# Neighbour marks instead of indices, one-hots on ScalarE, one softplus function, and three steps in other slots

## The chip, the cores and the metric

The kernel runs on one core of one Trainium2 chip. That core has TensorE (PE, matrix products), VectorE (DVE), ScalarE (ACT), GpSimd (POOL) and SyncE (SP), which here only starts transfers (DMAs). The engines run side by side, each through its own queue in order, and wait for each other by semaphores. The metric is the device time of one execution in microseconds (us). Three executions of the kernel before took 13008.24, 13020.53 and 13022.36 us; the median is 13020.53.

## The reference

The input is an image batch x of 16 x 96 x 64 x 64. Layer 0 is a graph convolution over windows of 8 x 8 pixels, layer 1 a stack of two Mamba blocks (state-space scans) over the 4096 pixels of each image, with a normalisation over the batch at the end. Cut to what matters here:

```python
# layer 0, in each window of 64 nodes
idx = knn_idx(nodes, 9)                       # the 9 nearest nodes of each node, itself included
feat = concat([x_i, x_j - x_i])               # for each neighbour j of i
h = gelu(affine(feat @ ew + eb)).max(axis=2)  # the greatest over the 9 neighbours
y = affine(conv1x1(h, fc2_w, fc2_b)) + x

# layer 1, twice for each image: one Mamba block
xs, z = split(layernorm(seq) @ in_w)
xc = silu(causal_conv4(xs) + conv_b)
dt, Bm, Cm = split(xc @ xproj_w)
delta = softplus(dt @ dt_w + dt_b)            # 192 channels
dA = exp(delta * A);  dBx = delta * Bm * xc   # 16 states per channel
h[l] = dA[l] * h[l-1] + dBx[l]
y = (sum_s h * Cm + Dp * xc) * silu(z)
seq = seq + y @ out_w
```

The order of the neighbours does not enter the result, since the maximum is taken over them.

## The kernel before, in words

**Items and slots.** Layer 1 is cut into 256 items: 16 images x 2 blocks x 8 pieces of 512 pixels. The states are taken two at a time (2 x 64 partitions), so an item has 8 slots, p = 0 to 7, each with 128 partitions x 3 x 512 values. The main loop (L871) writes 2048 slots one after the other. In each slot DVE does one scan (L911), adds the carried state to the first column (L907), and makes the input of the next slot's scan, db = u * bt (L734 in `times_b`). TensorE spreads B over the partitions (bt, L729 in `bcast`, into a single PSUM buffer), and sums the states into y (`folded`, L745 and L747). ACT makes da = exp(delta * A) two slots ahead (L708 in `chosen`), with four buffers of da. POOL multiplies the scan's result by C (L943). SP fetches C for each slot (ct, L701, in `chosen`, four buffers).

**Preparing an item.** `norm` and `prelude` are generators; the main loop runs one step of each per slot, up to the next `yield`. `norm(n + 2)` begins in slot 0 of item n, `prelude(n + 2)` in slot 4. The prelude's steps before the change are: the silu of half the convolution (slot 4), the other half and the gate's silus, then a load of the table with exp and ln (L627, slot 5); the product that holds dt, B and C, copied to `dbl` (slot 6); B and C sent off, the product for delta, its Abs and Relu (L653, L654, slot 7). In the next item: exp and 1 + exp (L656, L658), then ln (L661), minus one (L662) and the splitting of B into three bf16 parts (L665, L667), both in slot 0, which runs the prelude twice (L924, L925); then, on POOL, a correction and two sums that finish the softplus (L672, L674, L676, slots 1 to 3); `delta` is spread by eight DMAs of SP and u = delta * xc is formed on POOL (L679, L681, slot 4); u is spread by eight more DMAs (L684, slot 5). `doubled` issues these eight (L690, L692). Delta is first read by the small exps and by da of the next item's slot 0, which are written two slots ahead; u is first read by the db of the next item's slot 0, which is written in slot 7.

**Carry.** In slot 5 `carry(n + 1)` begins: a product on POOL (L717), an exp on ACT (L719), and in later slots a product with the carried state (L723), which L907 reads.

**Output.** In slot 6 `tail(n - 1)` begins: four matrix products of the gated result with out_w, plus the old sequence (L772 to L777), and a copy on ACT (L781).

**Layer 0.** Each image has 8 rows of 8 windows; a row is handled by `nearest` (distances and neighbours) and `edges` (products, gelu, maximum), also generators. The first four rows are done ahead of the main loop, the next ones quickly in the first items, the rest at one row per two items, in steps between the slots. In `nearest`, DVE finds the eight greatest of a row (L396) and their places (`max_index`, L397, run at the head of the next slot, at L909); SP writes the places to memory (L401). In `edges`, SP reads them back to 64 partitions (L430); POOL compares them with the partition's number for half of the windows (L441), and ACT does the same for the other half with an Abs and a Relu (L443, L444). The result is a one-hot matrix `oh`, with which PE picks the neighbours (L468, L471).

ACT holds one table of functions at a time. Silu, gelu and exp/ln are in different tables; before a function of another table an ACT_TABLE_LOAD stands in its queue.

Of the kernel before, what the change touches and what calls it, by code (L numbers as in the profile page):

```python
# [10 lines left out]
F32 = mybir.dt.float32  # L11
U16 = mybir.dt.uint16
BF16 = mybir.dt.bfloat16
AF = mybir.ActivationFunctionType
# [7 lines left out]
def tile_conv_knn_mamba(ctx: ExitStack, tc: tile.TileContext, w: dict, out: bass.AP):  # L22
# [44 lines left out]
    node = const.tile([NN, 1], F32, name="node")  # L67
    nc.gpsimd.iota(node, pattern=[[0, 1]], base=0, channel_multiplier=1, allow_small_or_imprecise_dtypes=True)
    minus_node = const.tile([NN, 1], F32, name="minus_node")
    nc.vector.tensor_scalar(minus_node, node, -1.0, None, ALU.mult)  # L70
# [237 lines left out]
    def half(h):  # L308
        return slice(h * CB, (h + 1) * CB)
# [21 lines left out]
    def nearest(b, q):  # L331
# [61 lines left out]
        idx = pr.tile([128, NP, KO], U16, tag="idx", name=f"idx_{nm}")  # L393
        for p in range(NP):
            m1 = pr.tile([128, KO], F32, tag="m1", name=f"m1_{nm}_{p}")
            nc.vector.max(m1, scs[:, p, :])  # L396
            opening.append(partial(nc.vector.max_index, idx[:, p, :], m1, scs[:, p, :]))  # L397
            yield SLOT

        idx_d = dram.tile([NP, 128, KO], U16, tag="idx_d", name=f"idxd_{nm}")  # L400
        nc.sync.dma_start(out=idx_d.rearrange("p i k -> i p k"), in_=idx)  # L401
        chosen_of[b, q] = idx_d
# [13 lines left out]
    def edges(b, q):  # L416
# [3 lines left out]
        idx_d = chosen_of.pop((b, q))  # L420
# [7 lines left out]
        for hf in range(2):  # L428
            idb = pr.tile([NN, NP, NN * KO], U16, tag="idb", name=f"idb_{nm}_{hf}", bufs=1)
            nc.sync.dma_start(  # L430
                out=idb.rearrange("j w n -> j (w n)"),
                in_=idx_d.rearrange("(s p) i k -> s (p i k)", s=2)[hf : hf + 1].to_broadcast([NN, NP * NN * KO]),
            )
            yield


            for p in (1, 0):
                ohj = ohs[p][0:NN].rearrange("j w i k -> j w (i k)")
                numbers = idb[:, 2 * p : 2 * p + 2, :]
                if p == 0:  # L440
                    nc.gpsimd.tensor_scalar(ohj, numbers, node, None, ALU.is_equal)  # L441
                else:
                    nc.scalar.activation(ohj, numbers, AF.Abs, bias=minus_node)  # L443
                    nc.scalar.activation(ohj, ohj, AF.Relu, bias=1.0, scale=-1.0)  # L444
                yield
# [119 lines left out]
    made = {}  # L565
    carried = {}
# [26 lines left out]
    def prelude(n):  # L593
# [31 lines left out]
        for part in range(2):  # L625
            project(z_in[i].unsqueeze(1), 1, part, z, 0.0)
        nc.scalar.preload_act_table_set("natural_log_exp_and_others")  # L627
# [13 lines left out]


        e = pr.tile([128, Q + QH], F32, tag="e", name=f"e_{nm}", bufs=1)
        rl = pr.tile([128, Q + QH], F32, tag="rl", name=f"rl_{nm}", bufs=1)
        va = pm.tile([128, Q], F32, tag="mm", name=f"pdta_{nm}")
        nc.tensor.matmul(va, lhsT=dt_w[i][:, :128], rhs=dbl, start=True, stop=True)
        vb = pm.tile([128, QH], F32, tag="mm", name=f"pdtb_{nm}")
        for h in range(2):
            nc.tensor.matmul(
                vb[half(h)], lhsT=dt_w[i][:, 128:], rhs=dbl[:, bass.ts(h, QH)], start=True, stop=True  # L650
            )
        for v, cols in ((va, slice(0, Q)), (vb, slice(Q, Q + QH))):
            nc.scalar.activation(e[:, cols], v, AF.Abs)  # L653
            nc.scalar.activation(rl[:, cols], v, AF.Relu)  # L654
        yield
        nc.scalar.activation(e, e, AF.Exp, scale=-1.0)  # L656
        s1 = pr.tile([128, Q + QH], F32, tag="s1", name=f"s1_{nm}", bufs=1)
        nc.scalar.activation(s1, e, AF.Identity, bias=1.0)  # L658
        yield
        ln = pr.tile([128, Q + QH], F32, tag="ln", name=f"ln_{nm}", bufs=1)  # L660
        nc.scalar.activation(ln, s1, AF.Ln)  # L661
        nc.scalar.activation(s1, s1, AF.Identity, bias=neg1)  # L662
# [9 lines left out]
        nc.gpsimd.tensor_tensor(e, e, s1, ALU.subtract)  # L672
        yield
        nc.gpsimd.tensor_tensor(ln, ln, e, ALU.add)  # L674
        yield
        nc.gpsimd.tensor_tensor(ln, ln, rl, ALU.add)  # L676
        yield
        delta = pr.tile([128, NB3, Q], F32, tag="delta", name=f"delta_{nm}")
        doubled(delta, ln)  # L679
        u = pr.tile([128, NB3, Q], F32, tag="u", name=f"u_{nm}")  # L680
        nc.gpsimd.tensor_tensor(s1, ln, xc, ALU.mult)  # L681
        made[n] = (xc, z, bp, c_d, delta, u)
        yield
        doubled(u, s1)  # L684
# [26 lines left out]
    def carry(n):  # L711
# [4 lines left out]
        d0 = made[n][4][:, :, 0:1].to_broadcast([128, NB3, NPR])  # L716
        nc.gpsimd.tensor_tensor(first, a_neg[i], d0, ALU.mult)  # L717
        yield
        nc.scalar.activation(first, first, AF.Exp)  # L719
# [151 lines left out]
    for m, (n, p) in enumerate(order):  # L871
# [17 lines left out]
        if p == 5 and k + 1 < NQ:  # L889
            going.append(carry(n + 1))  # L890
# [29 lines left out]
        if p == 6 and n:  # L920
            going.append(tail(n - 1))
        if p == 2:
            ahead()
        if p == 0:  # L924
            step_on(preps)  # L925
# [3 lines left out]
        held |= step_on(preps)  # L929
        close_steps()  # L930
# [83 lines left out]
```

## Time and profile before

| | |
|---|---|
| median of three runs | 13020.53 us |
| the profiled execution | 13021.43 us, its span 13019.7 us |
| mean granted clock of TensorE | 0.949 |
| first scan to last scan | begins at 263.3, the last at 12813.5 us |
| one item, in the middle of the run | 48.6 us, 8 slots |
| one item among the first five | about 76 us |
| DVE busy from 800 to 12800 us | 11431 of 12000 us |

In a line of a group the numbers after the shapes are the count, the busy time in us, the mean of one in ns, then how long the engine had been idle just before these instructions, and what ended most of that. A line of the waits has the engine that waited, the one it waited for, the total in us, how often, and the longest. In a line of the timeline stand the start and the length in us, the engine and line, the operation, and how many are merged; SPq is SP's queue as it issues a DMA, and its length there is the time to issue, not the time to land.

### The profile page before, as it was taken

Reading aid. Unit: us, or ns where it says so; the run is one execution under the profiler, and the core shown is the slowest. Engines: PE = TensorE matmul, PEld = TensorE weight load, DVE = VectorE, ACT = ScalarE, POOL = GpSimd, SP = SyncE. Lnnn points to the kernel's source line nnn. Section 1 sums busy time; section 2 is a strip of 40 time slices with the busy share of each in tenths; the row PEclk is TensorE's granted clock in tenths of the full one; section 3 lists DMA queues with packets and bytes.
Section 4 is the critical chain, followed back from the end, with each engine's and each line's share of the span. In section 5 each row is a group of like instructions: output and inputs, shape, how many; then the busy total and the mean of one; then the engine's idle time right before and its main releaser. Section 6 shows DMA issues by size and latency. Waiting matters only on the chain.

```text
span 13019.7 us, 155850 instructions
## 1 busy us (share of the span) xinstructions
PE 11254.7 (86%) x46920; PEld 4359.3 (33%) x46920; DVE 11940.4 (92%) x8270; ACT 10407.8 (80%) x16186; POOL 11686.0 (90%) x8644
## 2 busy tenths in 40 slices
PE   5889889888989989888888888988888888889872
PEld 2333333333333333333333333333333333333320
DVE  2699999999999999999999999999999999999995
ACT  4778888888888888888888888888888888888763
POOL 3699999999999999999999999999999999999993
PEclk8899999999999999999999999999999999999986
DMA  1233333333333333333333333333333333333336
GB/s 38 66 85 95 91 91 93 94 92 89 98 89 90 96 92 90 93 94 89 95 95 87 98 92 90 94 92 93 90 95 92 90 95 93 92 89 97 89 87 261
DMA packets 1031198, 1226.82 MB, mean 94 GB/s; under 512 B 429440, under 2 KB 560910, under 8 KB 1024208
## 3 DMA queue, kind: packets, MB, share of 16 engines
q1 hardware_dynamic: 1026352, 1191.59, 35.2%
q10 hardware_dynamic: 4000, 25.28, 0.5%
q8 instruction: 370, 6.06, 0.2%
q14 instruction: 476, 3.90, 0.1%
HBM read 706.83 MB, written 85.72 MB: 61 GB/s over the span
## 4 chain that ended last, share of the span: by engine, by line
POOL 27%; PE 19%; DVE 18%; ACT 13%; issue 9%; DMA 7%; SPq 6%; POOLq 0%; DVEq 0%; ACTq 0%
POOL hb L943 16%; DVE hb L911 11%; DVE db L734 6%; ACT da L708 5%; PE y L745 3%; SPq L690 2%; SPq L692 2%; DMA ct<-cd 2%; POOL ln L674 2%; PE t L468 2%; PE y L747 1%; PE pj L608 1%; PE t L471 1%; POOL hn L591 1%; POOL ln L676 1%
## 5 line engine op out<-in xcount | busy, mean ns | idle before, releaser
L943 POOL TENSOR_TENSOR hb<-hb,ct 128x1536 f32<-128x1536 f32 x2048 | 7091.9, 3463 | 313.5 <-DVE hb L911 78.4
L911 DVE TENSOR_TENSOR_SCAN hb<-da,db 128x1536 f32<-128x1536 f32 x2048 | 6863.5, 3351 | 216.6 <-ACT da L708 39.4
L708 ACT ACTIVATE da<-delta,a 128x511 f32<-128x511 f32 x6144 | 3937.7, 713 | 28.7 <-DVE hb L911 24.1
L734 DVE TENSOR_TENSOR db<-u,bt 128x1536 f32<-128x1536 f32 x2048 | 3605.3, 1760 | 386.6 <-PE bt L729 266.3
L745 PE MATMUL y<-hb,fold 128*64 128x512 f32 x8192 | 2273.8, 634 | 230.4 <-POOL hb L943 219.7
L476 ACT ACTIVATE da<-t,eb,es 128x512 f32<-128x512 f32 x1536 | 1181.3, 777 | 775.3 <-PE t L468 534.7
L747 PE MATMUL y<-hb,fold 128*64 128x256 f32 x8192 | 1259.5, 386 | 0.0
L729 PE MATMUL bt<-bparts,bsel 128*128 128x512 bf16 x2048 | 828.4, 404 | 462.4 <-DVE db L734 459.3
L468 PE MATMUL t<-oh,vu 128*128 128x512 f32 x2048 | 1012.8, 616 | 27.2 <-ACT da L476 14.1
L747 PEld LDWEIGHTS y<-hb,fold 128*64 128x64 f32 x8192 | 604.2, 141 | 1247.6 <-issue 1247.6
L413 DVE TENSOR_REDUCE hq<-da 128x192 f32<-128x1536 f32 x512 | 890.4, 1739 | 105.4 <-ACT da L476 105.4
L608 PE MATMUL pj<-hn,conv_in 128*128 128x512 f32 x2048 | 932.8, 598 | 0.9 <-POOL hn L591 0.9
L745 PEld LDWEIGHTS y<-hb,fold 128*64 128x64 f32 x8192 | 495.0, 141 | 1278.5 <-issue 528.6
L441 POOL TENSOR_SCALAR oh<-idb,node 64x1024 f32<-64x1024 uint16 x256 | 731.0, 2855 | 117.2 <-DMA idb<-idxd 111.6
L452 PE MATMUL pv<-ewT,y 96*64 96x192 f32 x2048 | 477.6, 360 | 335.2 <-ACT rs L588 253.4
L942 POOL COPY state<-hb 128x3 f32<-128x3 f32 x1792 | 397.5, 222 | 392.3 <-DVE hb L911 359.0
L620 ACT ACTIVATE xc<-pj,conv_b 128x512 f32<-128x512 f32 (+1 forms) x512 | 297.2, 580 | 510.5 <-PE pj L613 397.8
L471 PE MATMUL t<-oh,vu 128*64 128x512 f32 x2048 | 560.4, 626 | 167.0 <-ACT da L476 162.3
L608 PEld LDWEIGHTS pj<-hn,conv_in 128*128 128x128 f32 x2048 | 396.4, 194 | 386.5 <-issue 375.7
L613 PE MATMUL pj<-hn,conv_in 128*64 128x256 f32 x4096 | 514.4, 394 | 0.0
L452 PEld LDWEIGHTS pv<-ewT,y 96*64 96x64 f32 x2048 | 253.0, 143 | 774.4 <-ACT rs L588 358.4
L468 PEld LDWEIGHTS t<-oh,vu 128*128 128x128 f32 x2048 | 373.5, 194 | 402.9 <-issue 290.3
(180 smaller groups left out, 17972.0 us busy)
## 6 DMA issues: line engine op xcount, KB each, us to landing
ct<-cd SPq DMA_DIRECT2D x4096, 128.0 KB
delta<-ln SPq DMA_DIRECT2D x1024, 128.0 KB
u<-s SPq DMA_DIRECT2D x1024, 128.0 KB
idb<-idxd SPq DMA_DIRECT2D x256, 256.0 KB
delta<-ln SPq DMA_DIRECT2D x1024, 64.0 KB
u<-s SPq DMA_DIRECT2D x1024, 64.0 KB
x<-in_x SPq DMA_DIRECT2D x128, 192.0 KB
rn<-r4d SPq DMA_DIRECT2D x128, 192.0 KB
```

The costliest lines, as they stand in the source:

```text
L413: nc.vector.tensor_reduce(out(), g.rearrange("p s (i k) -> p s i k", k=KO), AX.X, ALU.max)
L441: nc.gpsimd.tensor_scalar(ohj, numbers, node, None, ALU.is_equal)
L468: nc.tensor.matmul(t, lhsT=vus[p][:, part, :128], rhs=ohw[part], start=True, stop=True)
L476: nc.scalar.activation(g, t, AF.Gelu, bias=e_b[:, j : j + 1], scale=e_s[:, j : j + 1])
L608: nc.tensor.matmul(ps, lhsT=wt[:, t, :128], rhs=hn[:, off : off + Q], start=(t == 0), stop=(t == taps - 1))
L708: nc.scalar.activation(da[:, c, 1:Q], delta[:, c, 1:], AF.Exp, scale=a_neg[i][:, c, p : p + 1])
L729: nc.tensor.matmul(bt, lhsT=bsel[:, p, :], rhs=made[n][2], start=True, stop=True)
L734: nc.vector.tensor_tensor(db, made[n][5], bt.unsqueeze(1).to_broadcast([128, NB3, Q]), ALU.mult)
L745: nc.tensor.matmul(y[half(h), 0], lhsT=fold, rhs=hb[:, h, :], start=False, stop=(p == NPR - 1))
L747: nc.tensor.matmul(y[half(h), 1, :QH], lhsT=fold, rhs=hb[:, 2, bass.ts(h, QH)], start=False, stop=(p == NPR - 1))
L911: nc.vector.tensor_tensor_scan(*(t.rearrange("p c q -> p (c q)") for t in (hb, das[at], db)), 0.0, ALU.mult, ALU.add)
L943: nc.gpsimd.tensor_tensor(hb, hb, ct.unsqueeze(1).to_broadcast([128, NB3, Q]), ALU.mult)
```

## The change

- **Neighbours as marks.** `max_index` becomes `match_replace`: DVE overwrites the eight greatest in the table of scores by a mark of 2^20. PE transposes the marked table by products with the identity (eight of 64 x 64 for a row of windows), and ACT makes it 0 or 1 in bf16 (`mt`). Nothing is written to memory and read back.
- **One-hots by ScalarE.** For each one-hot PE forms ranks: the number of marks before a node, by a product with a fixed triangular matrix, plus 100 for a mark itself, less 100 + k (`ranks`). Where that is zero the node is the k-th neighbour. ACT takes the Abs into `off`, and then Relu(1 - |.|), in two halves (`onehot`). POOL's comparison goes, and so do ACT's two passes over the places.
- **Softplus as one function.** `AF.Softplus` stands for the Abs, Relu, Exp, two Identity, Ln and the three POOL operations. It has a table of its own. `press` holds it, with its products and the eight DMAs of delta; it is run in slot 5, after the silus of the following prelude and ahead of the table load for exp and ln.
- **u** is then formed in slot 6 and spread in slot 7; the second prelude step in slot 0 goes.
- **Carry** begins in slot 6, and its POOL product and exp become three exps with a scale per partition.
- **The output projection** (`tail`) begins in slot 7.

```diff
@@ nearest
-            opening.append(partial(nc.vector.max_index, idx[:, p, :], m1, scs[:, p, :]))
+            opening.append(partial(nc.vector.match_replace, scs[:, p, :], m1, scs[:, p, :], MARK))
             yield SLOT
-        idx_d = dram.tile([NP, 128, KO], U16, tag="idx_d", name=f"idxd_{nm}")
-        nc.sync.dma_start(out=idx_d.rearrange("p i k -> i p k"), in_=idx)
-        chosen_of[b, q] = idx_d
+        ps = pm.tile([128, NP, NN], F32, tag="mm", name=f"mp_{nm}")
+        for h in range(2):
+            for p in range(NP):
+                nc.tensor.matmul(
+                    ps[half(h), p, :], lhsT=scs[half(h), p, :], rhs=ident[half(h), half(h)], start=True, stop=True
+                )
+        mt = pr.tile([128, NP, NN], BF16, tag="mt", name=f"mt_{nm}", bufs=3)
+        nc.scalar.activation(mt, ps, AF.Relu, bias=neg1, scale=2.0 / MARK)
+        chosen_of[b, q] = mt
@@ edges
-            idb = pr.tile([NN, NP, NN * KO], U16, tag="idb", name=f"idb_{nm}_{hf}", bufs=1)
-            nc.sync.dma_start(out=idb..., in_=idx_d...)
-            yield
-            for p in (1, 0):
...
-                if p == 0:
-                    nc.gpsimd.tensor_scalar(ohj, numbers, node, None, ALU.is_equal)
-                else:
-                    nc.scalar.activation(ohj, numbers, AF.Abs, bias=minus_node)
-                    nc.scalar.activation(ohj, ohj, AF.Relu, bias=1.0, scale=-1.0)
-                yield
+            def ranks(p):
+                ps = pm.tile([128, NN, KO], F32, tag="mm", name=f"rk_{nm}_{hf}_{p}")
+                nc.tensor.matmul(ps, lhsT=sel0, rhs=krow.rearrange("o (i k) -> o i k", k=KO), start=True, stop=False)
+                marks = mt[:, 2 * hf + p, :].unsqueeze(2).to_broadcast([128, NN, KO])
+                nc.tensor.matmul(ps, lhsT=before, rhs=marks, start=False, stop=True)
+                off = pr.tile([128, NN, KO], BF16, tag="off", name=f"off_{nm}_{hf}_{p}")
+                nc.scalar.activation(off, ps, AF.Abs)
+                return off
+            def onehot(p, off):
+                for h in range(2):
+                    nc.scalar.activation(ohs[p][0:NN, h], off[half(h)], AF.Relu, bias=1.0, scale=-1.0)
+            off = ranks(1)
+            yield
+            onehot(1, off)
+            off = ranks(0)
+            yield
+            onehot(0, off)
+            yield
@@ prelude
+        while pressed:
+            pressed.pop(0)()
         nc.scalar.preload_act_table_set("natural_log_exp_and_others")
...
-        for v, cols in ((va, slice(0, Q)), (vb, slice(Q, Q + QH))):
-            nc.scalar.activation(e[:, cols], v, AF.Abs)
-            nc.scalar.activation(rl[:, cols], v, AF.Relu)
-        yield
-        nc.scalar.activation(e, e, AF.Exp, scale=-1.0)
...
-        nc.gpsimd.tensor_tensor(e, e, s1, ALU.subtract)
-        yield
-        nc.gpsimd.tensor_tensor(ln, ln, e, ALU.add)
-        yield
-        nc.gpsimd.tensor_tensor(ln, ln, rl, ALU.add)
-        yield
...
-        doubled(delta, ln)
+        def press():
+            va = pm.tile([128, Q], F32, tag="mm", name=f"pdta_{nm}")
+            nc.tensor.matmul(va, lhsT=dt_w[i][:, :128], rhs=dbl, start=True, stop=True)
...
+            nc.scalar.activation(sp[:, :Q], va, AF.Softplus)
+            nc.scalar.activation(sp[:, Q:], vb, AF.Softplus)
+            doubled(delta, sp)
+        pressed.append(press)
-        nc.gpsimd.tensor_tensor(s1, ln, xc, ALU.mult)
         made[n] = (xc, z, bp, c_d, delta, u)
-        yield
-        doubled(u, s1)
+        for _ in range(5):
+            yield
+        while pressed:
+            pressed.pop(0)()
+        nc.gpsimd.tensor_tensor(up, sp, xc, ALU.mult)
+        yield
+        doubled(u, up)
@@ carry
-        nc.gpsimd.tensor_tensor(first, a_neg[i], d0, ALU.mult)
-        yield
-        nc.scalar.activation(first, first, AF.Exp)
+        delta = made[n][4]
+        for c in range(NB3):
+            nc.scalar.activation(first[:, c], a_neg[i][:, c], AF.Exp, scale=delta[:, c, 0:1])
@@ the main loop
-        if p == 5 and k + 1 < NQ:
+        if p == 6 and k + 1 < NQ:
             going.append(carry(n + 1))
...
-        if p == 6 and n:
+        if p == 7 and n:
             going.append(tail(n - 1))
...
-        if p == 0:
-            step_on(preps)
         held = step_on(going)
...
         held |= step_on(preps)
+        if p == 5:
+            while pressed:
+                pressed.pop(0)()
         close_steps()
```

## The prediction

> **What bounds the kernel now.** I read the page's busy times first, then its costliest groups, then the list of waits, then one item boundary in the timeline, engine by engine. An item is 8 slots; slot p of item n has one scan (L911). I write S5 for the start of the scan of slot 5.
>
> ```profile
> PE 11254.7 (86%) x46920; PEld 4359.3 (33%) x46920; DVE 11940.4 (92%) x8270; ACT 10407.8 (80%) x16186; POOL 11686.0 (90%) x8644
> L943 POOL TENSOR_TENSOR hb<-hb,ct 128x1536 f32<-128x1536 f32 x2048 | 7091.9, 3463 | 313.5 <-DVE hb L911 78.4
> L911 DVE TENSOR_TENSOR_SCAN hb<-da,db 128x1536 f32<-128x1536 f32 x2048 | 6863.5, 3351 | 216.6 <-ACT da L708 39.4
> L734 DVE TENSOR_TENSOR db<-u,bt 128x1536 f32<-128x1536 f32 x2048 | 3605.3, 1760 | 386.6 <-PE bt L729 266.3
> L441 POOL TENSOR_SCALAR oh<-idb,node 64x1024 f32<-64x1024 uint16 x256 | 731.0, 2855 | 117.2 <-DMA idb<-idxd 111.6
> ```
>
> VectorE (DVE) is the bound: scan 3.35 us and db 1.76 us in every slot. Between 800 and 12800 us it is busy 11431 of 12000 us, and what is idle there is mostly the 0.1 us between two of its instructions. The waits say the same:
>
> ```profile
> DVE db L734 <- PE bt L729: 266.3, 171, 14.2
> ...
> POOL oh L441 <- DMA idb<-idxd: 111.6, 13, 25.4
> ...
> DVE hb L911 <- ACT da L708: 39.4, 23, 6.4
> ```
>
> DVE's largest wait in its loop is 266.3 us, and 93.5 of that lies in the first 800 us. GpSimd (POOL) at 90% looks like a second bound, but it costs DVE almost nothing. So relief of POOL buys little; what lands on DVE's path costs its full length.
>
> Now one boundary, item 114 to 115 (S5 = 6000.05):
>
> ```profile
> 6000.05 3.34 DVE L911 TENSOR_TENSOR_SCAN hb<-da,db 128x1536 f32<-128x1536 f32 x1
> 6000.69 1.23 SPq L692 DMA_DIRECT2D delta<-ln  x2
> 6001.75 0.47 ACT L620 ACTIVATE xc<-pj,conv_b 128x256 f32<-128x256 f32 x1 [1.51 <-PE pj L613]
> 6002.67 1.17 SPq L690 DMA_DIRECT2D u<-s  x2
> 6002.86 0.92 ACT L620 ACTIVATE z<-pj 128x512 f32<-128x512 f32 x2 [0.63 <-PE pj L608]
> 6003.79 1.28 ACT L627 ACT_TABLE_LOAD   x1
> 6005.09 1.94 ACT L708 ACTIVATE da<-delta,a 128x511 f32<-128x511 f32 x3
> 6007.75 1.24 SPq L692 DMA_DIRECT2D u<-s  x2
> 6009.03 2.51 SPq L701 DMA_DIRECT2D ct<-cd  x4
> 6011.52 3.35 DVE L911 TENSOR_TENSOR_SCAN hb<-da,db 128x1536 f32<-128x1536 f32 x1
> 6014.97 1.76 DVE L734 TENSOR_TENSOR db<-u,bt 128x1536 f32<-128x1536 f32 x1
> ```
>
> The reader is to see three things. First, the db at 6014.97 (S5 + 14.9) is the first of item 115, and it needs all eight pieces of u. Second, SP issues big DMAs one after the other at 0.63 us each (two in 1.24, four in 2.51), and the eight of u ended at S5 + 8.9 here, at S5 + 6.1 in the median item: 6 to 9 us before they are needed, landing included. Third, the silus of slot 5 end at S5 + 3.7 here, S5 + 4.4 in the mean of items 6 to 242.
>
> **The change, part by part.**
>
> *One-hots.* It removes POOL's 256 comparisons (731.0 us), ACT's L443 and L444 (290.4 + 270.6), and SP's idxd and idb DMAs. It adds on ACT 512 Abs at 0.597 (as L653), 1024 Relu of 64x512 at some 0.56 (half of L444's 1.057 is the floor, L653's 0.597 the ceiling), and 128 marks at 0.371 (as L391): 306 + 573 + 47 = 926 us. On DVE 512 match-replaces stand for 512 FIND_INDEX8 of the same shape (0.218). Between MAX8's 0.202 and two FIND_INDEX8 that is -8 to +112 us; I take 0, by the nearest row. On PE come 1024 bf16 matmuls, at most 0.404 each (as L729), and 1024 of 64x64, at most 0.229 (as L389): at most 648 us, 2.5 per item. PE's idle time hides them, 13020 - 11255 = 1765 us, 6.9 per item; without that cover they cost their 2.5 per item (a rival below).
>
> *Softplus and carry.* POOL loses L672, L674, L676 and L717 (464.4 + 463.6 + 464.3 + 51.6). ACT loses L653, L654, L656, L658, L661, L662 and L719 (1443.8 us in all) and gains 512 softplus (0.597 and 0.392, as L653: 253 us), 672 small exps at 0.207 (139) and 256 table loads at 1.283 (328). So POOL falls by 2175 us to some 9500, and ACT by 2005 - 1646, to some 10050. Neither sets the end, so I count no gain for it except the DVE waits they feed.
>
> *The move.* This decides. Before, the softplus of an item began in slot 7 two items earlier; delta went out in slot 4 and u in slot 5 of the item before it. After, softplus runs in slot 5 of the item before it, behind the silus of the prelude of the item after it; delta's eight DMAs follow it at once; then, in SP's order, two ct of slot 7 and two ct of the next item's slot 0; u's product stands on POOL in slot 6, and its eight DMAs in slot 7, behind all these. The first db of the next item is written in the same slot 7. From S5:
> - silus end 4.5: the 4.4 of before, with up to 0.43 for the two rank matmuls ahead of them on PE, less what PE gains by being caught up.
> - table load to next instruction 1.30, first softplus 0.60: 6.4. A second load and two exps of the small carry follow on ACT; da of slot 7 is then done at 10.0 and needed at S7, 11.0 to 11.8: hidden.
> - SP: eight of delta 5.1 (median 5.03 from first to last), four ct 2.55, eight of u 5.1: 19.15. POOL's product is ready before that: hb of slot 5 ends near S5 + 7.1, the product takes 1.82, so 8.9, and u's turn on SP comes at 14.0.
> - The last u lands 2.4 after its issue ends (its median before; quartiles 1.75 and 3.0): 21.5.
>
> Needed at S5 + 14.85 (mean of the even items 14.47, of the odd 15.22). So DVE waits 6.65 us at each boundary. Nothing is behind DVE to absorb it, since every other engine waits for DVE's next db.
>
> Delta is second in line: it lands at 14.0, ACT's three exps of carry wait for it, and queued behind them on ACT stand dbl and da of the next slot 0, ready at 17.1. The scan wants them at 14.85 + 2.1 = 17.0. That wait alone would cost 0.1 us, and lies under u's.
>
> The output projection moves 2.6 us of PE and one ACT copy (0.566) from slot 6 to 7, where DVE now waits anyway: 0.
>
> *Sum.* 239 boundaries (items 6 to 244) x 6.65 = +1589. The last eleven have no layer-0 work, silus that end near 5.9 and db at 14.56: 22.9 - 14.56 = 8.3 each, +92. In the first items the slots are long (db at S5 + 28.8, silus to 11.1, u at 28.1): +4 in all. DVE's waits after the first 800 us are some 200 us; five of eight slots lie between the stall and the next S5, where PE and ACT are caught up: -110. The start loses the idxd and idb round trip (2.8 + 4.1, and 2.9 of POOL, against some 4 for transpose, ranks and Relu), about 6 us for some of the first nine rows, between 0 and 100: -50. Profiled execution 13021 + 1589 + 92 + 4 - 110 - 50 = 14546. That execution is 0.9 us over the median of the three runs (13020.5), so nothing is to be corrected; I say 14520.
>
> **Two rules against rows.** SP's rows put one issue at 0.63 us, twenty in a row at 12.8, against 2.4 to land. The Trainium skill, "DMA: Bandwidth & Descriptors", section "Issuing engines are not separate DMA queues", holds the time to initiate a DMA "usually small relative to the DMA itself", and its anatomy of one DMA (given for the gpsimd path) has about 0.05 us of dispatch; with that u would go out when POOL's product is ready, land near S5 + 12, and there would be no stall. The rows decide: here the issuing is the long part.
>
> ACT's rows show a table load followed by the next instruction 1.295 us after the load's start. The Trainium skill, "ScalarE: Activation LUTs", section "What ACT_TABLE_LOAD costs", asks 2.66 us for each switch, with a drain of 1.38, and its section on table sets says to batch calls by set, which speaks against a new set per item. By it the stall would be 8.0 us and the sum some 340 us higher; no row here shows that drain.
>
> **Rivals.**
> - *Faster: u is there in time.* The place is SP's queue between softplus and db; it decides if the last u lands before S5 + 14.85, that is at some 0.3 us per issue instead of 0.63. Then what is left are the waits: 200 us of DVE in the loop and some 50 in the start, so 12770 to 12900. Against it: 1024 issues of u at a median of 0.595 and gaps of 0.045.
> - *A smaller stall*, 1 to 4 us: the silus end sooner (the earliest of 240 items is 2.9) and the landing takes 1.75; 13021 + 250 x 2.5 = about 13650. For it: PE is idle during the stall and starts fresh. Against it: the silus wait for PE's products, and PE may not start slot 5 before DVE has read bt.
> - *PE becomes the bound*, with no stall by u: 2.5 us per item exposed is +640, half of it +320, so 13350. For it: PE at 86%. Against: that busy time is the modelled ends of pipelined matmuls.
>
> **How the numbers follow.** Forecast (stall of 4 to 8.5 us) 0.84, smaller stall 0.07, PE 0.03, faster 0.05, no change 0.01. The forecast's own ends: silus at 3.9 and landing 1.75 give 5.4 us, x 250 less 200, 14170; silus at 5.4 and landing 3.0 give 8.15, 14900. A lower clock adds up to 100: PE's granted clock falls from 0.97 to 0.85-0.91 where it has more gaps (after 12200 us). Toward the smaller stall I reach down to 13950. What a measurement tells from no change is about 0.2%; slower takes 0.84 + 0.07 + 0.03 = 0.94, faster 0.05, same 0.01.
>
> **What would show it.** Right: DVE's db (now L753) idle before some 250 times, 6 to 7 us each, put down to the DMA of u; item boundaries of 55 us instead of 48.6; DVE near 82%, POOL near 66%; u's issue ending some 19 us behind S5; no idle of ACT that reaches a scan. Wrong: u issued before slot 7's scan ends, or DVE still over 90%; then the order on SP or the place of the softplus is not what I read.

## The result, and the profile after

The changed kernel takes 14452.4 us (median; 14450.8 to 14456.0), the kernel before beside it 13021.4. The ratio is 1.1099, with a 95% interval of 1.108 to 1.1119: 11% slower. The profiled execution of the changed kernel has a span of 14449.1 us, 1429.4 more than before, and TensorE's granted clock is 0.914 in it, against 0.949.

The first view is the page of the changed kernel: busy time of each engine, then the groups of VectorE's two large instructions and of GpSimd's largest (count, busy us, mean ns, then the idle time just before them and what ended most of it).

```profile
PE 12005.4 (83%) x49992; PEld 4761.2 (33%) x49992; DVE 12012.7 (83%) x8282; ACT 10327.7 (71%) x16509; POOL 9622.7 (67%) x7397
L963 POOL TENSOR_TENSOR hb<-hb,ct 128x1536 f32<-128x1536 f32 x2048 | 7086.6, 3460 | 753.3 <-DVE hb L930 250.0
L930 DVE TENSOR_TENSOR_SCAN hb<-da,db 128x1536 f32<-128x1536 f32 x2048 | 6864.7, 3352 | 168.3 <-ACT da L728 16.9
L753 DVE TENSOR_TENSOR db<-u,bt 128x1536 f32<-128x1536 f32 x2048 | 3605.8, 1761 | 1817.9 <-DMA u<-up 1170.0
```

VectorE does the same work as before, 12012.7 us against 11940.4, but now in a span 1429 us longer. The idle time that is new stands before one instruction: db, 1817.9 us where it was 386.6. GpSimd has lost 2063 us of work, and nothing of it is seen in the end.

The list of waits of the changed kernel (engine and line, what it waited for, us in total, times, longest) says what db waits for:

```profile
DVE db L753 <- DMA u<-up: 1170.0, 191, 18.6
DVE db L753 <- DMA bs<-dbl: 435.6, 61, 15.7
DVE hq L432 <- ACT da L501: 94.8, 13, 26.0
DVE db L753 <- PE bt L748: 91.2, 66, 10.6
```

The second line is the same wait. db does not read bs; bs is the DMA that SP issues right after u, and where it was the last to land before db began, the wait is put down to it. Together they are 252 waits. Counted from VectorE's own instructions, the db of the next item's slot 0 waits over 1 us at 255 boundaries, 1627.7 us in all. The wait for bt, 266.3 us before, has shrunk to 91.2.

One boundary in the timeline of the changed kernel (start, length, engine and line; SPq is SP as it issues). S5, the start of slot 5's scan, is 6604.73:

```profile
6604.73 3.34 DVE L930 TENSOR_TENSOR_SCAN hb<-da,db 128x1536 f32<-128x1536 f32 x1
...
6606.85 0.92 ACT L646 ACTIVATE z<-pj 128x512 f32<-128x512 f32 x2 [0.63 <-PE pj L634]
...
6607.78 1.28 ACT L690 ACT_TABLE_LOAD   x1
...
6609.08 0.60 ACT L690 ACTIVATE sp<-pdta 128x512 f32<-128x512 f32 x1
...
6609.70 1.12 SPq L710 DMA_DIRECT2D delta<-sp  x2
...
6613.05 1.82 POOL L702 TENSOR_TENSOR up<-sp,xc 128x768 f32<-128x768 f32 x1
...
6614.76 2.46 SPq L721 DMA_DIRECT2D ct<-cd  x4
...
6617.33 1.17 SPq L710 DMA_DIRECT2D u<-up  x2
...
6621.11 1.24 SPq L712 DMA_DIRECT2D u<-up  x2
...
6624.07 1.76 DVE L753 TENSOR_TENSOR db<-u,bt 128x1536 f32<-128x1536 f32 x1 [4.89 <-DMA u<-up]
```

Read it downwards as one chain. The silus end at S5 + 3.0, the load and the first softplus at S5 + 5.0. From 6609.70 to 6622.35 SP issues twenty DMAs without a pause: eight of delta, four ct, eight of u, 12.65 us, 0.63 each. GpSimd's product, which u needs, is done at 6614.87, 2.5 us before SP comes to u. The last issue of u ends at S5 + 17.6, and db starts 1.7 us later. VectorE finished the scan of slot 7 at 6619.18 and stood for 4.9 us. This item waits less than most: over items 20 to 239 the last issue of u ends at S5 + 19.6 in the mean, and the wait is 6.2 us. The first db starts at S5 + 20.3 in even items and at S5 + 22.3 in odd ones, against 14.5 and 15.2 before.

### The profile page after: what moved, and what is told of

Same layout as the page of the kernel before. It is cut to its first block, busy times and chain, and to the rows that moved or that the text cites. A ratio compares the mean times of both kernels' runs of the same rounds, so it can differ in the third digit from the quotient of the medians.

```text
span 14449.1 us, 159686 instructions
## 1 busy us (share of the span) xinstructions
PE 12005.4 (83%) x49992; PEld 4761.2 (33%) x49992; DVE 12012.7 (83%) x8282; ACT 10327.7 (71%) x16509; POOL 9622.7 (67%) x7397
## 4 chain that ended last, share of the span: by engine, by line
PE 26%; POOL 21%; DVE 13%; ACT 12%; issue 11%; SPq 10%; DMA 7%; DVEq 0%; POOLq 0%; ACTq 0%
POOL hb L963 15%; DVE hb L930 7%; DVE db L753 6%; SPq L710 4%; SPq L712 4%; ACT da L728 4%; PE y L764 4%; PE pj L634 4%; PE t L493 3%; PE t L496 2%; DMA u<-up 2%; PE bt L748 2%; PE pj L639 2%; SPq L721 2%; DMA bs<-dbl 2%
## 5 line engine op out<-in xcount | busy, mean ns | idle before, releaser
L753 DVE TENSOR_TENSOR db<-u,bt 128x1536 f32<-128x1536 f32 x2048 | 3605.8, 1761 | 1817.9 <-DMA u<-up 1170.0
L728 ACT ACTIVATE da<-delta,a 128x511 f32<-128x511 f32 x6144 | 3945.5, 710 | 29.3 <-DVE hb L930 20.3
L764 PE MATMUL y<-hb,fold 128*64 128x512 f32 x8192 | 2511.0, 671 | 28.1 <-POOL hb L963 28.1
L766 PE MATMUL y<-hb,fold 128*64 128x256 f32 x8192 | 1412.3, 403 | 0.0
L609 ACT ACTIVATE sqv<-pc 96x512 f32<-96x512 f32 x256 | 151.6, 592 | 1532.8 <-PE pc L607 1532.7
L766 PEld LDWEIGHTS y<-hb,fold 128*64 128x64 f32 x8192 | 680.2, 149 | 1337.9 <-issue 1337.9
L764 PEld LDWEIGHTS y<-hb,fold 128*64 128x64 f32 x8192 | 611.7, 150 | 908.3 <-issue 615.2
L477 PE MATMUL pv<-ewT,y 96*64 96x192 f32 x2048 | 603.5, 433 | 98.3 <-ACT sqv L609 80.6
L462 ACT ACTIVATE oh<-off 64x512 f32<-64x512 bf16 x1024 | 639.4, 624 | 7.0
L478 PE MATMUL pv<-ewd,y 96*64 96x192 f32 x2048 | 603.0, 433 | 0.0
L672 POOL CAST b<-bs 128x64 bf16<-128x64 f32 x768 | 181.5, 236 | 588.5 <-DMA bs<-dbl 555.7
L702 POOL TENSOR_TENSOR up<-sp,xc 128x768 f32<-128x768 f32 x256 | 465.3, 1817 | 149.4 <-ACT sp L691 149.4
```

Source lines behind the costliest of these rows:

```text
L728: nc.scalar.activation(da[:, c, 1:Q], delta[:, c, 1:], AF.Exp, scale=a_neg[i][:, c, p : p + 1])
L753: nc.vector.tensor_tensor(db, made[n][5], bt.unsqueeze(1).to_broadcast([128, NB3, Q]), ALU.mult)
L764: nc.tensor.matmul(y[half(h), 0], lhsT=fold, rhs=hb[:, h, :], start=False, stop=(p == NPR - 1))
L766: nc.tensor.matmul(y[half(h), 1, :QH], lhsT=fold, rhs=hb[:, 2, bass.ts(h, QH)], start=False, stop=(p == NPR - 1))
```

## The experiments

All times are medians. The kernel before, run beside each group, took 13019.7 us (first four), 13029.9 (fifth to eighth), 13029.7 (ninth to eleventh) and 13033.9 us (twelfth).

### u two DMAs earlier in SP's order

```diff
         nc.gpsimd.tensor_tensor(up, sp, xc, ALU.mult)
-        yield
         doubled(u, up)
```

> The changed kernel with one thing moved: u is spread in slot 6, right after its product, so that its eight DMAs stand ahead of the two ct of the next item's slot 0 in SP's queue and not behind them. Nothing is added or taken away. Theory (the issuing on SP sets the end): two issues of 0.64 us less between the softplus and the last u, 1.28 us less of wait at each of 250 boundaries, 320 us, so about 14130 us and a mean wait of db at the boundary of 4.9 us instead of 6.2. Rival (u is late because the softplus or POOL's product is late, and SP only follows): no change, 14400 to 14450. Rival (the boundary is held by delta and ACT's da, u merely ends near it): less than 100 us.

Measured: 14125.2 us (14112.6 to 14133.3), ratio 1.0848 (1.0832 to 1.0865), 327 us less than the changed kernel. With the step gone, u's eight DMAs stand ahead of the two ct of the next item's slot 0. Two issues of 0.63 us are 1.26; the wait at the boundary fell from 6.22 to 4.97 us in the mean of items 6 to 244, by 1.25. Nothing else was moved, so it is SP's order that sets the end, to the length of one issue. The wait is still put down to u:

```profile
DVE db L752 <- DMA u<-up: 1154.0, 233, 7.5
```

### Softplus early, in the item's own preparation

```diff
+        nc.scalar.activation(sp[:, :Q], va, AF.Softplus)
+        nc.scalar.activation(sp[:, Q:], vb, AF.Softplus)
+        nc.scalar.preload_act_table_set("natural_log_exp_and_others")
...
-        for _ in range(5):
+        for _ in range(3):
             yield
-        while pressed:
-            pressed.pop(0)()
+        doubled(delta, sp)
         nc.gpsimd.tensor_tensor(up, sp, xc, ALU.mult)
```

> The changed kernel with the softplus function where the Exp stood before (in slot 0, in the prelude's own step, with a table load before it and one behind it), delta spread in slot 4 and u in slot 5 as in the kernel before. Marks, ranks and one-hots, carry and the output projection stay as changed. It has one table load more per item than the changed kernel. Theory (only the place of the softplus and its DMAs costs): the boundary waits go, 6.2 us at 250 items and some 60 us in the first six, so 12780 to 12950 us, a little faster than the kernel before, since POOL and the waits on it are relieved. Rival (the added matmuls make PE the bound): 13250 to 13650. Rival (the table loads on ACT cost): 256 x 1.28 = 330 us more, 13200.

Measured: 13385.9 us (13381.2 to 13390.5), ratio 1.028 (1.0266 to 1.0294). The stall is gone: no db at a boundary after item 6 waits over half a microsecond, and 1066 of the 1432 us are back. But the expectation, a time below that of the kernel before, failed: 366 us remain, in other places:

```profile
DVE db L748 <- PE bt L743: 404.0, 310, 10.2
DVE hb L925 <- ACT da L723: 143.7, 142, 4.8
DVE hb L925 <- PE y L761: 118.5, 82, 3.2
```

These are VectorE's largest waits in this run. Most of them lie in slots 2 to 4, above all of the even items, and all hang on TensorE and ScalarE: before, bt cost 266.3 us, da 39.4 and y 29.2. So something else in this kernel costs time in slots 2 to 4. The next runs look for it, first in the marks, and the last of them finds it elsewhere.

### The marks alone

The kernel before with the marks, ranks and one-hots by ScalarE of the change; softplus, carry and output projection stay as they were.

> The kernel before with the neighbour part of the change alone (marks, transposes, ranks, one-hots on ACT); softplus, delta, u, carry and output projection stay as before. Theory: about 731 us less on POOL and the DMA round trip gone, which DVE feels only in its waits (200 us in the loop, some 90 in the start): 12850 to 13000 us. Rival (PE): up to 2.5 us per item, 13350 to 13650. Rival (ACT, which gains some 365 us of work): 13100 to 13300.

Measured: 13734.1 us (13718.9 to 13760.2), ratio 1.0556 (1.0542 to 1.0571). A clear miss, above both rivals too: the marks alone cost 714 us. The waits in this run:

```profile
DVE db L759 <- PE bt L754: 850.2, 476, 10.5
POOL e L697 <- ACT s L687: 746.1, 244, 6.6
...
PEld pow L797 <- ACT off L456: 460.8, 237, 2.3
...
PE pow L797 <- ACT off L456: 347.9, 237, 1.8
```

VectorE waits 850 us for bt, which needs only VectorE's own release of its buffer and TensorE's turn. TensorE in its turn waits for ScalarE's Abs of the ranks (off), before the output projection (pow), 237 times. The wait of the matmuls (PE) lies within that of their weight loads (PEld), so it is 461 us in all. Ranks and projection use the same two PSUM buffers, and a buffer is free only when ScalarE has come to the Abs.

### Softplus, carry and projection alone

The kernel before with the rest of the change and without the marks; ScalarE's Gelu stands in for softplus.

> The kernel before with the other part of the change alone: one function in slot 5 behind the silus, u in slot 7, carry in slot 6, output projection in slot 7; neighbours and one-hots stay as before. The one function is Gelu in place of Softplus, which changes what delta holds and keeps the table loads (1305, the changed kernel has 1309) and the sizes. Theory: the stall at the boundary is all here: 14300 to 14600 us, with a wait of db at the boundary of 5.5 to 7 us. Rival (the one-hot part causes it): about 13000 us.

Measured: 14180.1 us (14175.9 to 14192.4), ratio 1.0893 (1.0876 to 1.0909). That is 120 us below the expected range, and the wait below the expected 5.5 to 7 us. But the stall belongs to this part: 5.28 us at a boundary in the mean of items 6 to 244, put down to the DMA of u in the waits:

```profile
DVE db L728 <- DMA u<-up: 1181.9, 212, 18.1
```

The two parts cost 1160 and 714 us alone and 1432 together: beside the new softplus the marks cost 272 us and not 714. By these figures most of the 272 go through the head of the chain. Without the marks the silus end at S5 + 2.8 in even and 4.1 in odd items, with them at 3.7 and 5.6, 1.2 us later in the mean; the boundary waits 0.94 us longer, which over 239 boundaries is 225 us.

### What in the marks costs: three kernels

First, the marks with the projection in slot 7, as the change has it:

```diff
-        if p == 6 and n:
+        if p == 7 and n:
             going.append(tail(n - 1))
```

> The marks alone (13,734 us), with one line more of the change: the output projection starts in slot 7 and not in slot 6. Theory A, the cost of the marks is order on TensorE: the projection's first matmul (L797) waits 461 + 348 us for the Abs of the ranks (L456), because both write the same two PSUM buffers, and the next bt stands behind it in TensorE's queue (VectorE's wait in slot 1 of even items: 346 us). Then most of these waits go and the time falls by 250 to 400 us, to 13,330-13,490. Theory B, the cost is the work that the marks add (ranks on TensorE 495 us, Abs and Relu on ScalarE 937 us): the time stays within 60 us of 13,734.

Measured: 13621.4 us (13612.2 to 13645.9), ratio 1.0451 (1.0433 to 1.0468), 113 us less. The wait of the projection for the Abs is gone from the list, 461 us of TensorE's idle time, but VectorE's wait for bt only went from 850.2 to 758.6. Part of it moved: the db of slot 1 in even items waits some 115 us more. Neither theory had it; the named wait was real, and taking it out gave back a sixth of the 714 us.

Second, no rank matmuls; third, rank matmuls that nobody reads:

```diff
-                ps = pm.tile([128, NN, KO], F32, tag="mm", name=f"rk_{nm}_{hf}_{p}")
-                nc.tensor.matmul(ps, lhsT=sel0, ...)
-                nc.tensor.matmul(ps, lhsT=before, rhs=marks, ...)
-                nc.scalar.activation(off, ps, AF.Abs)
+                nc.scalar.activation(off, krow.rearrange("o (i k) -> o i k", k=KO), AF.Abs)
```

(The third keeps the first three lines.)

> The marks alone, and the 1024 rank matmuls are left out: the Abs reads a constant row in SBUF in place of the ranks, so that the neighbours' one-hots are not the reference's. ScalarE's work stays (937 us), TensorE loses 495 us of matmuls and weight loads, and no Abs holds a PSUM buffer. Theory A (PSUM buffers held until ScalarE gets to the Abs): 13,250-13,450. Theory B with TensorE as its engine: 13,050-13,250. Theory B with ScalarE as its engine: 13,600-13,750.

> As the run before, but the rank matmuls are issued and their result is not read by the Abs, which reads the constant row (the one-hots are again not the reference's). So TensorE's work is that of the marks, and a buffer comes free as soon as TensorE has written it. Theory A: as the run before, within 100 us of it, since it is the holding that costs. Theory B with TensorE's work: 350 us or more above the run before, near 13,700.

Measured: without ranks 13209.3 us (13209.2 to 13214.1), ratio 1.0138 (1.0121 to 1.0155); unread 13405.1 us (13400.3 to 13413.8), ratio 1.0289 (1.0272 to 1.0306). VectorE's wait for bt in these two, in this order:

```profile
DVE db L729 <- PE bt L724: 463.9, 323, 10.5
```

```profile
DVE db L733 <- PE bt L728: 619.4, 375, 10.9
```

Without ranks the time is in the range of theory B with TensorE, below that of theory A. Unread ranks then cost 196 us, more than the 100 of theory A and less than the 350 of theory B. So both causes are there, and neither theory had that. The 714 us of the marks come apart like this: 13734 - 13405 = 329 go with ScalarE's reading the ranks from the shared PSUM buffers (buffers held, Abs waiting for TensorE), 13405 - 13209 = 196 for the matmuls themselves, and 13209 - 13030 = 179 for the rest, in which are the Abs and Relu on ScalarE and the 64x64 products of the marks. (The first of these differences is taken across two groups, whose runs of the kernel before differ by 10 us.)

### Softplus as ln(1 + exp), nothing else

```diff
-            nc.scalar.activation(e[:, cols], v, AF.Abs)
-            nc.scalar.activation(rl[:, cols], v, AF.Relu)
+            nc.scalar.activation(e[:, cols], v, AF.Exp)
...
-        nc.scalar.activation(ln, s1, AF.Ln)
-        nc.scalar.activation(s1, s1, AF.Identity, bias=neg1)
+        nc.scalar.activation(ln, e, AF.Ln, bias=1.0)
...
-        nc.gpsimd.tensor_tensor(e, e, s1, ALU.subtract)
-        nc.gpsimd.tensor_tensor(ln, ln, e, ALU.add)
-        nc.gpsimd.tensor_tensor(ln, ln, rl, ALU.add)
```

(The exp of -|v| and the 1 + e between them go too; every yield stays where it was.)

> The kernel before, with softplus as two functions, ln(1 + exp(v)), in the same slots of the prelude: GpSimd loses 3 x 464 = 1392 us, ScalarE 930 us, no table load and no DMA is added or moved, and the one-hots are as before. If the ends of VectorE's short waits before (db for bt 266 us, the scan and the folds for ScalarE and GpSimd some 200) hang on these two engines: 12,750-12,950, faster than both kernels. If VectorE's own work and TensorE alone set the end: 13,000-13,040, no change, and then GpSimd's relief is worth nothing by itself.

Measured: 12868.8 us (12867.5 to 12873.9), ratio 0.9875 (0.9858 to 0.9891): 161 us faster than the kernel before, and 1584 us faster than the changed one. It needs no table load of its own, no other place in ScalarE's queue and no DMA moved. What it gains is in VectorE's short waits:

```profile
DVE db L726 <- PE bt L721: 160.8, 106, 14.3
```

Before, this was 266.3 us in 171 waits. From item 6 on, VectorE's waits over 0.2 us sum to 78 us, boundaries included, where they were 233; hardly any are left to gain.

### Early softplus again, as ln(1 + exp)

```diff
-        nc.scalar.activation(sp[:, :Q], va, AF.Softplus)
-        nc.scalar.activation(sp[:, Q:], vb, AF.Softplus)
-        nc.scalar.preload_act_table_set("natural_log_exp_and_others")
+        nc.scalar.activation(sp[:, :Q], va, AF.Exp)
+        nc.scalar.activation(sp[:, Q:], vb, AF.Exp)
+        nc.scalar.activation(sp, sp, AF.Ln, bias=1.0)
```

> As the run in which softplus stood early in the item's own prelude (13,386 us, marks and all else as changed), but with softplus as ln(1 + exp(v)), which needs none of the 1024 - 512 extra table loads. Theory A, what that run had missed was the marks (TensorE's and ScalarE's order in slots 0 to 4; the marks with the projection in slot 7 cost 591 us alone, ln(1 + exp) gave 161 alone): 13,300-13,450, as before within 90 us. Theory B, it was ScalarE's table loads in the early slot (two of 1.29 us in half of the items and one in the rest, some 400 us): 12,950-13,150.

Measured: 13031.8 us (13027.2 to 13041.7), ratio 1.0002 (0.9992 to 1.0011): no change against before, 354 us less than with the softplus function. Theory B's direction holds, and its size nearly, though its count of the loads was short: the second experiment's trace has 512 of them around the softplus, two per item and 657 us:

```profile
L679 ACT ACT_TABLE_LOAD x256 | 328.4, 1283 | 153.3 <-PE pdta L673 153.2
L681 ACT ACT_TABLE_LOAD x256 | 328.4, 1283 | 4.6
```

The waits of this run, to be set beside those of the second experiment:

```profile
DVE db L748 <- PE bt L743: 282.0, 205, 10.5
...
DVE hb L925 <- ACT da L723: 40.0, 21, 4.8
```

Everything of the change but the function and its place is in this kernel, the marks too, and there is no stall. All of that together costs 163 us over the kernel with ln(1 + exp) alone. So the marks' 714 us are no fixed price: beside a softplus that takes ScalarE less time, and with the projection in slot 7, the marks and whatever the other parts cost or gain come to 163. Which difference does it was not taken apart.

### The changed kernel with u issued by two engines

```diff
-                nc.sync.dma_start(out=t[half(h), k, :], in_=src[half(k), :Q])
+                queues[h].dma_start(out=t[half(h), k, :], in_=src[half(k), :Q])
...
-        doubled(u, up)
+        doubled(u, up, (nc.sync, nc.scalar))
```

> The changed kernel, with four of the eight DMAs of u issued by ScalarE and four by SP. Theory SP (the stall is the time in which SP issues, 0.63 us each): the last issue comes 4 x 0.63 = 2.5 us earlier, the wait at the boundary falls from 6.2 to 3.7 us, 250 times: 13,830, and up to 14,200 if ScalarE's exps come late by its wait for the product and its own four issues. Rival (the stall is the transfers' bytes or their landing time, which two queues share): within 60 us of 14,452.

Measured: 14639.5 us (14631.5 to 14657.4), ratio 1.1236 (1.1217 to 1.1255): slower than the changed kernel by 187. The forecast failed, and the timeline of this run shows how. S5 of this item is 6595.84:

```profile
6609.60 0.49 ACTq L710 DMA_DIRECT2D u<-up  x1
...
6611.70 1.26 SPq L712 DMA_DIRECT2D u<-up  x2
...
6612.32 0.48 ACTq L710 DMA_DIRECT2D u<-up  x1
...
6614.07 1.22 ACTq L712 DMA_DIRECT2D u<-up  x2
...
6617.77 1.76 DVE L753 TENSOR_TENSOR db<-u,bt 128x1536 f32<-128x1536 f32 x1 [7.87 <-DMA ct<-cd]
```

SP was done with its four at 6612.96, S5 + 17.1. ScalarE's four stand in its queue in order, each between exps and copies, and the last ended at 6615.29, S5 + 19.5. db started 2.5 us after that. It is the same in all of items 20 to 239: SP ends its four at S5 + 17.1 in the mean, 2.5 us sooner than in the changed kernel, as theory SP had it, but ScalarE is always last and ends at 19.6, as late as SP alone did. And db starts 2.6 us after the last issue, where it was 1.7; so the wait at the boundary grew to 7.07 us. Why the last part takes 0.8 us longer stays open. A second queue helps only if its engine is free at that moment, and ScalarE is not.

### Eight more DMAs ahead of u

```diff
+        spare = dram.tile([8, CB, Q], F32, tag="spare", name=f"spare_{nm}")
+        for r in range(8):
+            nc.sync.dma_start(out=spare[r], in_=up[half(r % 2), :Q])
         doubled(u, up)
```

> The changed kernel, with eight more DMAs per item ahead of those of u on SP: the product of 64 x 512 f32 into a scratch area in DRAM that nobody reads. Theory SP: 8 x 0.63 = 5.0 us more at each of some 245 boundaries, 1,235 us: 15,500-15,800. Rival (SP's issuing is hidden and the wait is for the landing of the transfers): within 200 us of 14,452.

Measured: 15816.5 us (15806.2 to 15819.4), ratio 1.214 (1.212 to 1.216), 1364 us more than the changed kernel and 16 above the top of the expected range. The wait at the boundary went from 6.22 to 11.45 us, by 5.23. In the timeline, where the scan of slot 5 starts at 6615.74:

```profile
6630.05 5.04 SPq L706 DMA_DIRECT2D spare<-up  x8
...
6638.98 1.24 SPq L715 DMA_DIRECT2D u<-up  x2
...
6641.83 1.76 DVE L756 TENSOR_TENSOR db<-u,bt 128x1536 f32<-128x1536 f32 x1 [12.03 <-DMA u<-up]
```

Eight issues take 5.04 us, and that is what the boundary pays, though nobody waits for these eight. The rival, in which SP's issuing is hidden, is out. So is the thought that db waits for the bytes of the DMAs ahead of u: in the mean of items 20 to 239 the last issue of u ends at S5 + 18.3 with u two DMAs earlier, at 19.6 in the changed kernel and at 24.8 here, and db starts 1.7 to 1.8 us after it in all three.

### Two table loads that nobody needs

```diff
+        nc.scalar.preload_act_table_set("softplus_and_others")
+        nc.scalar.preload_act_table_set("natural_log_exp_and_others")
         nc.scalar.activation(sp[:, :Q], va, AF.Exp)
```

> The early softplus as ln(1 + exp(v)) (13,032 us), with two table loads that nothing needs put ahead of its exps: the set of softplus, and the set of exp and ln again. So ScalarE gets 512 loads of 1.283 us, 657 us in all, at the place where the run with the one softplus function has them. If the loads are what separates that run (13,386 us) from this kernel: 13,300-13,450. If it is something else in the softplus function or in its place in ScalarE's queue: 13,030-13,130.

Measured: 13410.2 us (13399.5 to 13430.1), ratio 1.0293 (1.0276 to 1.031), 378 us more than without the two loads and 24 from the kernel with the softplus function. The waits are near that kernel's again:

```profile
DVE db L750 <- PE bt L745: 391.6, 300, 10.0
DVE hb L927 <- PE y L763: 168.1, 103, 3.3
DVE hb L927 <- ACT da L725: 134.6, 135, 4.8
```

So it is the loads, 657 us of ScalarE's time, for which the early softplus function pays some 370 us at the end. That closes what the second experiment left open, to some 24 us.

## Why the prediction was right, and where its terms were off

**The bound and the mechanism were right.** VectorE is the bound, and the chain of silus, softplus, delta's DMAs, ct and u's DMAs sets each boundary. Moving two issues gave 1.25 us back, adding eight took 5.23 more, taking the softplus out of the chain removed the stall. The steps from S5, in means of items 20 to 239 where nothing else is said:

- Silus end: 4.5 predicted; 3.7 in even and 5.6 in odd items, 4.65 together. The kernel before had 4.4 and 4.45.
- Load and softplus: 1.9 predicted, 1.30 + 0.60 measured in the item shown.
- SP: twenty issues, 12.75 predicted, 13.0 measured (12.65 in the item shown). The last ends at 19.6, predicted 19.15.
- The product of u before its turn: 8.9 against 14.0 predicted; 10.0 against 14.4 measured (10.1 against 12.6 in the item shown).
- From the last issue's end to db: 2.4 predicted as the landing, 1.7 measured. The semaphore updates of the kernel before give 1.7 in the median for its last u as well (2.3 from the issue's start), so the 2.4 was read too long.
- First db: 21.5 predicted, 21.3 measured. That it is so near is partly luck: issues that end 0.4 us later and a landing that is 0.7 us shorter nearly cancel.
- Delta's readers: da of the next slot 0 was predicted for 17.1, 0.1 us late by itself. In the item shown it is done at S5 + 13.4, so nothing of it would show.

**The sum, term by term.** The measured values are differences of VectorE's waits of over 0.2 us before db and its other instructions, of its busy time, and of the start of the first scan, between the two profiled executions.

| term | predicted us | measured us |
|---|---|---|
| boundaries of items 6 to 244 | 239 x 6.65 = 1589 | 1486.5 - 1.3 = 1485 (6.22 each) |
| the last boundaries | 92 | 59 (ten of 5.9) |
| the boundaries before | 4 | 35 |
| VectorE's other waits, from item 6 | -110 | 72 - 231 = -159 |
| the start | -50 | -13 to the first scan, -47 in items 0 to 5 |
| VectorE's own work | 0 | 72 |
| sum | 1525 | 1432 |

The span grew by 1429.4; the 3 us between are idle times too short to be counted here. The forecast of 14520 was 68 us above the measured 14452, and the largest part is the stall itself, mis-sized by 0.43 us: the first db starts 0.2 us earlier than predicted (21.3), and without its wait of 6.2 it would have started at 15.1, 0.25 later than the "needed at S5 + 14.85". The 14546 that the prediction's terms come to, against its starting 13021, were written down as 14520. The last boundaries were ten and not eleven, and each waits 5.9 us, not 8.3. VectorE's other waits lost more than was counted. The prediction's reason, that TensorE and ScalarE stand caught up after each stall, is not shown: ln(1 + exp) alone takes them from 231 to 76 us with no stall at all. Two terms that did not reach the end were off as well. ScalarE's busy time fell by 80 us and not by some 360, among other things since the one-hots take 996 us and not 926 and the small exps 191 and not 139; GpSimd's fell by 2063 and not 2175.

**Which step failed though the total did not show it.** "PE's idle time hides them", and with it 0 for the one-hots. Beside the new softplus the marks cost 272 us, most of it by the later silus: the prediction had bounded their delay by 0.43 us, and it is 1.2. The total did not show it, by luck: without the marks the rest of the change ends the silus at 3.4 in the mean, against 4.4 before, earlier by nearly as much. Whether that comes from the stall, after which TensorE is caught up, or from ScalarE's lighter work stays open; with ln(1 + exp) alone, without a stall, they end at 2.8 in even and 4.5 in odd items. Beside the old softplus the marks cost 714 us. The rival with TensorE as the bound had named 320 to 640 us for them without a stall, with a chance of 3 in 100; of its mechanism, exposed matmuls, the runs show 196 us, and 329 belong to the Abs and the buffers that they hold.

**"Relief of POOL buys little"** held: the run with ln(1 + exp) took 1317 us from GpSimd and 769 from ScalarE, and gained 161 by both together. The rival "faster" had named 12770 to 12900 for a kernel without stall and with fewer waits, and that run is at 12869. With u in time and the softplus function kept, the kernel came to 13386: that rival had not counted what the table loads cost.

**The output projection's move at 0:** beside the stall that was not measured by itself. With the marks alone it is worth 113 us.

**The two rules.** SP's rows put an issue at 0.63 us, and the run with eight more DMAs shows 5.23 us at the boundary for them. The Trainium skill, "DMA: Bandwidth & Descriptors", section "Issuing engines are not separate DMA queues", says that issuing from several engines at once only saves the sequencer's time, which is "usually small relative to the DMA itself". The run with two engines agrees that it saves only this: SP was done 2.5 us sooner, and no time came of it. That it is small does not hold here, where twenty issues, 12.65 us in the item shown, stand against 1.7 us of landing after the last, and the issuing decides.

A table load is followed by the next instruction 1.30 us after its start (6607.78 to 6609.08 above). The Trainium skill, "ScalarE: Activation LUTs", section "What ACT_TABLE_LOAD costs", asks 2.66 us for a switch, 1.38 of it a drain; the load itself, 1.28 us, is what the rows here have, and no run here shows the drain. By the last experiment, 512 loads of 1.283 us added 378 us to the end, 0.74 us each.

**What showed it.** Predicted were some 250 waits of 6 to 7 us (255, 6.2 in the mean from item 6), items of 55 us (54.4), VectorE near 82% (83), GpSimd near 66% (67) and u's issue ending some 19 us behind S5 (19.6 in the mean, 17.6 in the item shown).

## What to carry to other kernels

A queue that only starts transfers is an engine like the others: sum its issues from the moment when the first becomes possible to the moment when the last is needed, and see what stands ahead in its order. Work that is "hidden in idle time" has to be looked up in the slot where it lands: the same marks cost 714 us beside the old softplus and 272 beside the new one, and two table loads per item cost 378 us on an engine that is busy 78% of the time. And when a long sequence is to be shortened, a form that uses the functions already loaded (here exp and ln) can be worth more than a single function that needs another table and another place.

## What the runs showed of the hardware that was not expected

- ScalarE's table loads hurt although ScalarE is busy only 78% of the span without them: 657 us of loads in the early slot, 378 us at the end. VectorE's waits for bt and da rise from 282.0 and 40.0 us to 391.6 and 134.6.
- ScalarE issues a DMA of 64 x 512 f32 in 0.47 us (median), where SP takes 0.59, but in its own order, between its activations.
- TensorE's granted clock falls with the stall: 0.949 before and 0.963 with the early ln(1 + exp), both without one, 0.914 with 6.2 us per item, 0.879 with 11.5.
- The addition before the maximum of layer 0 (128 x 768 f32 on VectorE, 128 times) took 954 ns in the mean before and 1486 ns in the changed kernel, 68 us in all: most of the 72 us of VectorE's own work above.

```profile
L507 DVE TENSOR_TENSOR hq<-hq,sa 128x768 f32<-128x768 f32 x128 | 122.1, 954 | 0.2
```

```profile
L532 DVE TENSOR_TENSOR hq<-hq,sa 128x768 f32<-128x768 f32 x128 | 190.2, 1486 | 0.2
```

The trace of the changed kernel points at the moved product of u. There 59 of the 128 lie mostly beside that product on GpSimd and take 1902 ns in the mean; 16 with GpSimd idle take 935. Before, and with the softplus part alone (1008 ns), none lies beside it. No run was made for it, so the cause is argued and not shown.
